# A graph layer: more columns copied by VectorE and ScalarE, and a wider repeated sum

## The chip, the core and the metric

The kernel runs on one core of one Trainium2 chip. The metric is the device time of one execution in microseconds. Five engines work beside each other and meet only through semaphores: PE (TensorE, matmuls; PEld is its weight load), DVE (VectorE), ACT (ScalarE), POOL (GpSimd), which here only issues gathers, and SP (SyncE), which only issues DMAs. A matmul writes PSUM, and only ACT and DVE read it out.

## What is computed

One layer of a graph network, a residual sum and a layer norm, for 12500 nodes of 64 numbers and 212500 edges, sorted by their destination, with 32 numbers each:

```
msg_in     = concat(nodes[src], nodes[dst], edge_features)      # 64 + 64 + 32
messages   = relu(msg_in @ mW1 + mb1) @ mW2 + mb2               # hidden width 128
aggregated = segment_sum(messages, dst)
u          = relu(concat(nodes, aggregated) @ uW1 + ub1) @ uW2 + ub2
out        = layernorm(nodes + u)
```

All of it is float32.

## The kernel before

The edges are cut into 554 groups of 384 (G), a group into three tiles of 128 (TG). Since the edges are sorted, the destinations of a group lie in a window of 32 nodes (W), whose start the kernel reads into a register.

Each group goes through three parts, and each part is matmuls on PE followed by reads of PSUM on ACT or DVE.

- **turn** (lines 354 to 379): the source rows of each tile, gathered by POOL into `own_s`, stand beside a one-hot of 32 columns for the place in the window, made by DVE (line 324). PE transposes both (line 360), and ACT copies the result into the block `own_st` (line 372), counting the edges of each place on the way.
- **hidden** (lines 381 to 409): PE multiplies the turned columns by `own_wm`, the first weights with the window's 32 rows in the middle (line 392), and ACT applies the relu into `own_h` (line 401).
- **sums** (lines 411 to 436): PE multiplies the hidden values of each tile by the one-hot (line 422), which adds them up by node: 128 hidden numbers by 32 nodes. The one-hot is broadcast four times (TIMES), so that PE makes the same 32 columns four times beside each other, 128 columns in all; only the first 32 are read. DVE adds them into `agg` (line 431) and the counts into a row of `xc` (line 432).

A float32 matmul is two instructions in the trace, each with a weight load.

The order is written out by hand. Iteration k (line 536) issues one step with turn(k), hidden(k-2) and sums(k-4), in this order on PE. Only the last matmul of a step raises PE's semaphore, and ACT and DVE wait for it. A step uses the PSUM buffer of k modulo 2, so step k+2 waits for what ACT and DVE read of step k. In each fourth step, those with k a multiple of 4, a further matmul (line 310) prepares the window rows of the next four groups and is then the last of its step; DVE copies the rows out (line 315, four copies). The last ten groups (SHORT) are issued part by part.

DVE's own order in an iteration is: the one-hot of group k+1, the adds of the step, and then column copies (below). So the one-hot that step k+2 needs is queued behind the column copies of iteration k.

**Gathers.** POOL gathers the rows of a tile with one indirect DMA (line 145). `own_s` is a ring of 20 groups; the gathers of a group wait for ACT's turn copy of the group 20 before. Iteration k issues those of group k+16.

**Column copies.** For some groups the third tile is not gathered. Instead its 128 source nodes are copied one column after the other out of `xc`, which holds all nodes transposed in SBUF, into a buffer `own_f`. `BY_DVE` lists the groups for which DVE does it (line 349), every 16th from 44: 31 groups. `BY_ACT` lists those of ACT (line 350), every 24th from 48: 21 groups. The 128 copies are spread over the 16 or 24 iterations that end 3 before the group is turned, 8 or 5.33 an iteration; the column numbers are read into eight registers at a time, one register load (line 343) for each eight copies. The hidden part of such a group has four matmul instructions in place of two for that tile: 64 rows from `own_f` padded with zeros, and the rest of the rows apart.

All 52 of these groups have numbers that are multiples of 4.

Updates of finished nodes (lines 438 to 485) are put between the steps, 512 nodes at a time.

Of the kernel before, what the change touches and what calls it, by code (L numbers as in the profile page):

```python
# [22 lines left out]
D = 64  # L23
# [5 lines left out]
W = 32  # L29
TG = 3  # L30
GE = TG * P
G = (E + GE - 1) // GE
# [11 lines left out]
NEAR_GROUPS = 24  # L44
SHORT = 10
ONE = TG - 1
BY_DVE = range(44, G - 16, 16)
BY_ACT = range(48, G - 16, 24)
COPIED = {**dict.fromkeys(BY_DVE, (ET.DVE, BY_DVE)), **dict.fromkeys(BY_ACT, (ET.Activation, BY_ACT))}
SLACK = 3  # L50
REGS = 8
TIMES = 4


def tiles_of(g):

    n = min(GE, E - g * GE)
    return [min(P, n - j * P) for j in range((n + P - 1) // P)]
# [23 lines left out]
class Own:  # L82
# [4 lines left out]
    def __init__(self, nc, ctx):  # L87
        def on(name, *shape, of=nc.sbuf_tensor):
            return ctx.enter_context(of(name, list(shape), F32)).ap()
# [6 lines left out]
        self.f = {way: [on(f"own_f{len(way)}_{i}", P, P) for i in range(2)]  # L96
                  for way in (BY_DVE, BY_ACT)}
        self.ident = on("own_ident", P, P)
# [6 lines left out]
def ordered(ctx: ExitStack, tc: tile.TileContext, a, own, ok):  # L105
# [25 lines left out]
    def after(first, *others):  # L131

        tc.declare_no_dep(first.ins, group="quiet", reason="waits for the last of a step")
        for i in others:
            tc.add_manual_dep(
                first.ins, i.ins.name,
                mybir.DependencyInfo(mybir.DependencyClass.Sync, mybir.DependencyReason.DATA),
                reason="the kernel's own rings",
            )
        return first  # L140
# [165 lines left out]
    def windows(b, wp, own_bank=True):  # L306


        xw, n = xws.pop(b)
        did = nc.tensor.matmul(wp[: n * W, :], xw[:, :n, :], w1b, start=True, stop=True)  # L310

        def copies():
            for i in range(n):
                g = b * SB + i
                c = nc.vector.tensor_copy(wm[g % NW][D : D + W, :], wp[i * W : (i + 1) * W, :])  # L315
                after(c, *([did] if own_bank else []), *([hidden_by[g - NW]] if g >= NW else []))
                wm_by[g] = c

        return did, copies
# [91 lines left out]
    def sums(g, ps):  # L411
        h, s = own.h[g % NH], own.s[g % RING]
        sizes = tiles_of(g)
        sg = ps[:, 2, : TIMES * W].rearrange("p (t w) -> p t w", w=W)


        lo = D if sizes[-1] == P else 0
        line = ps[0:1, 2, TIMES * W :][:, : D + W - lo]
        did = [nc.tensor.transpose(line, counts[lo:, g : g + 1], ident[lo : D + W, lo : D + W])]  # L419
        line = line[:, D - lo :]  # L420
        for j, p in enumerate(sizes):
            did.append(nc.tensor.matmul(  # L422
                sg, h[:p, j, :],
                s[:p, j, D:].unsqueeze(1).to_broadcast([p, TIMES, W]),
                start=j == 0, stop=j == len(sizes) - 1))

        def add(step):
            sums_by[g] = step
            at = bass.ds(starts.pop(g), W)
            return [  # L430
                after(nc.vector.tensor_tensor(agg[:, at], sg[:, 0, :], agg[:, at], ALU.add), step),  # L431
                after(nc.vector.tensor_tensor(xc[D : D + 1, at], line,  # L432
                                              xc[D : D + 1, at], ALU.add), step),
            ]

        return did, [*relu_by[g], copy_by[g]], add
# [53 lines left out]
    def step_update(g):  # L490
# [5 lines left out]
        elif now:  # L496
            got = now[1](now[0])
            now = [got, *now[2:]] if len(now) > 2 else []

    users = {part: [[], []] for part in (turn, hidden, sums)}  # L500

    def step(*work):
# [10 lines left out]
        for part, g, *_ in parts:  # L513
            if part is sums:
                for b in [b for b in xws if (b - 1) * SB <= g][:1]:
                    last, copies = windows(b, own.ps[g % 2][:, 2, (TIMES + 1) * W :][:, :H])
                    did.append(last)
# [18 lines left out]
    for k in range(G):  # L536
        if k < BITS:
            bit(k)
        if k % SB == 2:
            inputs(k // SB + 2)  # L540
        if k % SB == 1:
            places(k // SB + 1)
        onehot(k + 1)
        if k < G - SHORT:
            step((turn, k), *([(hidden, k - 2)] if k > 1 else []),
                 *([(sums, k - 4)] if k > 3 else []))
            made, summed = max(0, k - 1), max(0, k - 3)
        else:

            step((turn, k))  # L550
            for _ in range(2):
                if summed < made:
                    step((sums, summed))
                    summed += 1
            for _ in range(2):
                if made <= k:
                    step((hidden, made))
                    made += 1
        if k + AHEAD < G:
            gather(k + AHEAD)  # L560
        copies_of(k)
# [334 lines left out]
```

## Time and profile before

| | us |
|---|---|
| median of three runs | 2691.51 (2681.98 to 2695.5) |
| the profiled execution | 2690.72 |
| its span, first to last instruction | 2688.9 |
| mean granted clock of TensorE | 0.787 |

The span leaves 1.8 us of the profiled execution outside it. In that execution PE is busy 63% of the span, POOL 57%, DVE 39% and ACT 31%, so none is full. In the lines of the profile, L422 is line 422 of the kernel. A group line gives the line, the engine, the operation, output<-input, the count, the busy time and the mean of one in ns, and then the idle time of that engine just before such instructions and what ended it. A timeline line gives the start and the length in us; several equal instructions in a row are merged (x6), and the bracket names the idle time before the first. "issue" is idle time for which the profile shows no wait, and "remote" is a wait whose end the profile cannot name. The granted clock is 1.0 or 0.5 at each moment.

### The profile page before, as it was taken

The page shows a single profiled execution, that of the slowest core. Times are in us where ns is not written, and L with a number is a line of the kernel's source. Part 1 is how long each engine was busy: PE and PEld are TensorE (multiplying, and loading weights), DVE is VectorE, ACT ScalarE, POOL GpSimd, SP SyncE. Part 2 cuts the span into 40 slices and gives each one's busy share as a digit, 9 for nine tenths or more (in the row PEclk, how much of TensorE's full clock was granted, in tenths as well). Part 3 has the DMA queues.
Part 4 walks back from the last instruction along what each step waited for, and adds up shares of the span by engine and source line. Part 5 has one row for each costly group of instructions (what it writes and reads, how often), then busy time and mean ns, then how long its engine had stood idle before and what let it go on. Part 6 is the DMA issues. An engine that isn't in the chain of part 4 may idle for free.

```text
span 2688.9 us, 45023 instructions
## 1 busy us (share of the span) xinstructions
PE 1687.1 (63%) x9545; PEld 1457.1 (54%) x9545; DVE 1060.2 (39%) x7163; ACT 827.3 (31%) x4455; POOL 1519.4 (57%) x1616
## 2 busy tenths in 40 slices
PE   1356666666666675766666656666566666677667
PEld 0355555555555565655555555555555555565555
DVE  4124344344443444443434434434344343443423
ACT  0123333333333333333333333333333333333322
POOL 7565555555555555555555555555555555565550
PEclk9777787778777777777777878787777777787779
DMA  3211111111111111111111111111111111111110
GB/s 80 58 44 32 35 32 36 31 36 32 35 37 32 34 34 35 31 36 32 37 31 35 34 32 34 34 34 34 35 32 34 33 37 31 35 35 35 33 34 14
DMA packets 71878, 95.29 MB, mean 35 GB/s; under 512 B 32633, under 2 KB 40076, under 8 KB 71596
## 3 DMA queue, kind: packets, MB, share of 16 engines
q0 software_dynamic: 51488, 52.80, 10.3%
q1 hardware_dynamic: 19193, 39.06, 5.3%
q8 instruction: 81, 1.33, 0.2%
q14 instruction: 202, 1.65, 0.2%
q10 hardware_dynamic: 914, 0.46, 0.1%
HBM read 88.90 MB, written 3.20 MB: 34 GB/s over the span
## 4 chain that ended last, share of the span: by engine, by line
PE 50%; issue 18%; another core or an unknown queue 16%; ACT 10%; ACTq 3%; DVE 3%; DMA 0%; DVEq 0%; SPq 0%
PE own_ps L422 19%; PE own_ps L392 16%; PE own_ps L360 9%; ACT own_h L401 3%; ACT own_f L350 3%; ACT own_st L372 3%; ACTq L343 2%; PE own_ps L419 2%; PE u_ps L462 2%; PE u_ps L449 1%; PE own_ps L310 1%; ACTq L350 1%; PE u_ps L450 1%; DVE agg L431 1%
## 5 line engine op out<-in xcount | busy, mean ns | idle before, releaser
L145 POOL DMA_INDIRECT own_s<-in_x,src_sb x1609 | 1518.6, 944 | 1091.0 <-ACT own_st L372 677.1
L360 PE MATMUL own_ps<-own_ident,own_s 128*96 128x128 f32 x1661 | 364.2, 341 | 906.5 <-issue 677.0
L372 ACT ACTIVATE own_st<-own_ps 96x384 f32<-96x384 f32 (+2 forms) x606 | 286.1, 472 | 1697.7 <-PE own_ps L422 1006.0
L360 PEld LDWEIGHTS own_ps<-own_ident,own_s 128*96 128x96 f32 x1661 | 224.4, 159 | 983.9 <-issue 735.6
L422 PE MATMUL own_ps<-own_s,own_h 128*128 128x128 f32 x3322 | 647.5, 343 | 0.4 <-issue 0.3
L392 PE MATMUL own_ps<-own_wm,own_st 128*128 128x128 f32 (+1 forms) x3322 | 630.8, 338 | 1.4 <-DVE own_wm L315 1.4
L392 PEld LDWEIGHTS own_ps<-own_wm,own_st 128*128 128x128 f32 (+1 forms) x3322 | 571.9, 251 | 16.5 <-issue 11.7
L431 DVE TENSOR_TENSOR agg<-own_ps,agg 128x32 f32 x554 | 105.2, 190 | 1202.7 <-ACT own_h L401 1089.6
L422 PEld LDWEIGHTS own_ps<-own_s,own_h 128*128 128x128 f32 x3322 | 525.6, 236 | 27.3 <-issue 0.3
L349 DVE COPY own_f<-xc 64x1 f32 x3968 | 428.8, 143 | 217.7 <-issue 213.2
L350 ACT ACTIVATE own_f<-xc 64x1 f32 x2688 | 304.6, 193 | 9.1 <-issue 6.2
L401 ACT ACTIVATE own_h<-own_ps 128x384 f32<-128x384 f32 x553 | 263.3, 476 | 18.4 <-PE own_ps L392 13.1
L315 DVE COPY own_wm<-own_ps 32x128 f32<-32x128 f32 x550 | 156.9, 285 | 6.8 <-issue 1.3
L324 DVE TENSOR_TENSOR own_s<-iota,dlc 128x96 f32<-128x96 f32 x554 | 135.7, 245 | 21.6 <-issue 16.7
L432 DVE TENSOR_TENSOR xc<-own_ps,xc 1x32 f32 x554 | 101.2, 183 | 27.8 <-PE u_ps L450 7.4
L419 PE MATMUL own_ps<-own_ident,own_counts 32*1 32x32 f32 x554 | 107.1, 193 | 4.2 <-ACT own_st L372 1.9
L372 ACT ACTIVATION_READ_ACCUMULATOR own_st<-own_ps 96x1 f32 (+1 forms) x554 | 106.4, 192 | 0.6
L303 DVE COPY xw<-xc 66x32 f32 x554 | 78.6, 210 | 49.2 <-issue 48.3
L419 PEld LDWEIGHTS own_ps<-own_ident,own_counts 32*1 32x1 f32 x554 | 41.3, 74 | 93.8 <-issue 47.8
L310 PE MATMUL own_ps<-w1b,xw 66*128 66x128 f32 (+1 forms) x276 | 56.9, 290 | 0.0
L462 PE MATMUL u_ps<-u,u 128*128 128x64 f32 (+1 forms) x196 | 49.1, 398 | 10.0 <-ACT u L452 10.0
L462 PEld LDWEIGHTS u_ps<-u,u 128*128 128x128 f32 (+1 forms) x196 | 47.5, 326 | 11.5 <-ACT u L452 11.3
(63 smaller groups left out, 338.5 us busy)
## 6 DMA issues: line engine op xcount, KB each, us to landing
own_st<-in_efT SPq DMA_DIRECT2D x138, 192.0 KB
own_s<-in_x,src_sb POOLq DMA_INDIRECT x1609
xin<-in_x SPq DMA_DIRECT2D x24, 128.0 KB
out<-o SPq DMA_DIRECT2D x24, 128.0 KB
xc<-in_xT SPq DMA_DIRECT2D x12, 179.2 KB
dlc_i<-in_dst_cols SPq DMA_DIRECT2D x1, 831.0 KB
xc<-in_xT SPq DMA_DIRECT2D x4, 179.5 KB
src_sb<-in_src SPq DMA_DIRECT2D x13, 50.5 KB
```

The costliest lines, as they stand in the source:

```text
L145: nc.gpsimd.indirect_dma_start(out=s[:p, j, :D], out_offset=None, in_=x[:, :], in_offset=bass.IndirectOffsetOnAxis(ap=src_sb[:p, g * TG + ...
L315: c = nc.vector.tensor_copy(wm[g % NW][D : D + W, :], wp[i * W : (i + 1) * W, :])
L324: places_by[g] = nc.vector.tensor_tensor(own.s[g % RING][:, :, D:], iota.unsqueeze(1).to_broadcast([P, TG, W]), dlc[:, g * TG : (g + 1) * ...
L349: c = (nc.vector.tensor_copy(*column) if engine == ET.DVE else nc.scalar.activation(*column, AF.Copy))
L350: else nc.scalar.activation(*column, AF.Copy))
L360: nc.tensor.transpose(xt[:, j * P : j * P + p], s[:p, j, :], ident[:p, :p])
L372: nc.scalar.activation(t[to, c : c + m], xt[to, :m], AF.Copy, **({"accum_out": counts[to, g : g + 1]} if to.stop > D else {})), step)
L392: did.append(nc.tensor.matmul(pre[:p, j, :], edges, weights, start=i == 0, stop=i == len(parts) - 1))
L401: relu_by[g] = [nc.scalar.activation(h, pre, AF.Relu)]
L419: did = [nc.tensor.transpose(line, counts[lo:, g : g + 1], ident[lo : D + W, lo : D + W])]
L422: did.append(nc.tensor.matmul(sg, h[:p, j, :], s[:p, j, D:].unsqueeze(1).to_broadcast([p, TIMES, W]), start=j == 0, stop=j == len(sizes) - 1))
L462: nc.tensor.matmul(o_ps[:p, k], u[:, k:q:n], u2, start=True, stop=True)
```

## The change

```diff
-BY_DVE = range(44, G - 16, 16)
-BY_ACT = range(48, G - 16, 24)
+BY_DVE = range(44, G - 16, 12)
+BY_ACT = range(50, G - 16, 12)
 COPIED = {**dict.fromkeys(BY_DVE, (ET.DVE, BY_DVE)), **dict.fromkeys(BY_ACT, (ET.Activation, BY_ACT))}
 SLACK = 3
 REGS = 8
-TIMES = 4
+TIMES = 8
+FEW = 4
...
     def sums(g, ps):
         h, s = own.h[g % NH], own.s[g % RING]
         sizes = tiles_of(g)
-        sg = ps[:, 2, : TIMES * W].rearrange("p (t w) -> p t w", w=W)
+        times = TIMES if g < G - SHORT else FEW
+        sg = ps[:, 2, : times * W].rearrange("p (t w) -> p t w", w=W)
...
             did.append(nc.tensor.matmul(
                 sg, h[:p, j, :],
-                s[:p, j, D:].unsqueeze(1).to_broadcast([p, TIMES, W]),
+                s[:p, j, D:].unsqueeze(1).to_broadcast([p, times, W]),
                 start=j == 0, stop=j == len(sizes) - 1))
```

With G = 554 the new ranges hold 42 groups for DVE and 41 for ACT. DVE's are still multiples of 4; ACT's are 2 above a multiple of 4. Each engine's 128 copies are now spread over 12 iterations, 10.67 an iteration. The sums' matmuls have 256 columns in place of 128, but in the last ten groups, where they keep 128. The counts' row and the window rows move to later columns of the same PSUM bank.

## Prediction

> **What bounds it.** I first read the page's chain of the work that ended last and its costliest groups. Columns of a group line: line, engine, operation, output<-input, count | busy us, mean ns | idle before, releaser.
>
> ```profile
> PE 50%; issue 18%; another core or an unknown queue 16%; ACT 10%; ACTq 3%; DVE 3%; DMA 0%; DVEq 0%; SPq 0%
> L145 POOL DMA_INDIRECT own_s<-in_x,src_sb x1609 | 1518.6, 944 | 1091.0 <-ACT own_st L372 677.1
> L422 PE MATMUL own_ps<-own_s,own_h 128*128 128x128 f32 x3322 | 647.5, 343 | 0.4 <-issue 0.3
> L349 DVE COPY own_f<-xc 64x1 f32 x3968 | 428.8, 143 | 217.7 <-issue 213.2
> L350 ACT ACTIVATE own_f<-xc 64x1 f32 x2688 | 304.6, 193 | 9.1 <-issue 6.2
> ```
>
> The chain runs through PE for half the span, and for 16% through a wait that the profile can't name. Yet POOL's own row adds up to the span: 1518.6 busy and 1091.0 idle are 2609.6 us, and its last gather starts at 2610. Then the list of waits, for what POOL's idle time is:
>
> ```profile
> ACT own_st L372 <- PE own_ps L422: 1006.0, 245, 8.2
> POOL own_s L145 <- ACT own_st L372: 677.1, 274, 8.7
> ACT own_st L372 <- remote: 487.5, 78, 20.0
> ```
>
> POOL stops 274 times for ACT's turn copy, 2.47 us each, after 1609/274 = 5.9 gathers: two groups. So POOL does six gathers, stops with its ring full, and is freed by two turn copies. Third, the timeline of one such round of four groups:
>
> ```profile
> 1490.16 0.49 ACT L372 ACTIVATE own_st<-own_ps 96x384 f32<-96x384 f32 x1 [5.96 <-remote]
> 1491.01 0.94 POOL L145 DMA_INDIRECT own_s<-in_x,src_sb  x1 [2.40 <-ACT own_st L372]
> 1492.69 0.85 DVE L349 COPY own_f<-xc 64x1 f32 x8
> 1494.52 0.26 DVE L324 TENSOR_TENSOR own_s<-iota,dlc 128x96 f32<-128x96 f32 x1
> 1494.88 0.85 PE L360 MATMUL own_ps<-own_ident,own_s 128*96 128x128 f32 x3 [6.75 <-issue]
> ...
> 1496.00 0.94 POOL L145 DMA_INDIRECT own_s<-in_x,src_sb  x1 [0.30 <-issue]
> 1497.08 1.34 PE L422 MATMUL own_ps<-own_s,own_h 128*128 128x128 f32 x6
> 1498.45 0.49 ACT L372 ACTIVATE own_st<-own_ps 96x384 f32<-96x384 f32 x1 [5.48 <-PE own_ps L422]
> 1499.30 0.94 POOL L145 DMA_INDIRECT own_s<-in_x,src_sb  x1 [2.36 <-ACT own_st L372]
> 1503.63 0.39 PE L310 MATMUL own_ps<-w1b,xw 66*128 66x128 f32 x2
> 1505.54 0.94 POOL L145 DMA_INDIRECT own_s<-in_x,src_sb  x1 [0.30 <-issue]
> 1508.03 0.87 ACT L372 ACTIVATE own_st<-own_ps 64x256 f32<-64x256 f32 x2 [6.10 <-remote]
> ```
>
> The round has two halves. **Half A** (1490.16 to 1498.45): ACT frees PSUM, DVE works through adds, window rows and column copies up to the one-hot at 1494.52, PE begins at 1494.88 after 6.75 us of idleness, and ACT starts 0.03 us after PE's last sum. POOL had stopped by then, so this chain is on the path. **Half B** (1498.45 to 1508.03): PE's step ends with L310 at 1504.02, but ACT starts 4.0 us later. It starts 2.49 us after POOL's last gather began; of 205 such starts that came over 0.5 us after PE's end, the median is 2.42, half of them within 2.35 to 2.48. I can't say why ACT's release comes only with the end of POOL's burst; I take it as the trace shows it: half B lasts as long as POOL's six gathers and their landing, and PE has slack there.
>
> I counted this for groups 40 to 535. Steps k = 2 modulo 4 (half A): in 73 of 124 ACT starts within 0.1 us of PE's end (no slack), in the other 51 on average 1.26 us later. Steps k = 0 modulo 4 (half B): 3.43 us later on average, 2% without slack.
>
> **The change, part by part.** The sum is made against the profiled execution, 2690.72 us, which is 0.8 below the median of 2691.51, so no correction is due.
>
> *Fewer gathers.* 52 become 42 + 41 = 83 copied groups, so 31 gathers go (and 31 DMAs of POOL's queue). One costs 0.94 + 0.30 = 1.25 us of POOL's time (1491.01, 1492.26, 1493.50 in the timeline). What counts is in which half they go. A group's gathers wait for the turn copy 20 groups before, so groups 0 and 1 modulo 4 are gathered in half A, 2 and 3 in half B. All 52 were in A. Now DVE's 42 are in A and ACT's 41 in B. In B, where POOL is the limit: -41 x 1.25 = **-51 us**. In A 10 gathers more would cost 12 us if POOL limited it, but there the chain is late: 0.
>
> *DVE.* An iteration copies 10.67 columns in place of 8. Eight take 0.96 us, 0.145 the last, so one each 0.116: +0.31 us. Register loads rise from 1 to 1.33 an iteration; one takes 0.608 us (L343 on DVE's queue) and nothing runs on DVE meanwhile, with about 0.65 between copies: +0.21. Together 0.52 us ahead of the one-hot. In A it is on the path, in B below the slack.
>
> *ACT.* 5.33 become 10.67 copies of 0.097 (x6 take 0.66), loads of 0.55 rise from 0.67 to 1.33: +0.9 us an iteration. They stand behind the relu, so PE's next step does not wait; the second turn copy of a pair does, which POOL needs 3.75 us after the first and has now after some 1.4. Hidden; without that cover 0.9 us a half. No wait is added: the copies of a group begin 15 iterations before it, into a buffer whose last reader, the hidden part of the group 24 before, was issued seven iterations earlier.
>
> *Sums.* The trace has no 256-column matmul. Six of 128 columns begin 0.213 us apart at half clock and 0.112 at full clock (L392 x6 takes 1.49 and 0.83). The nearest row that is wider is the update's, with 512 columns, at half clock:
>
> ```profile
> 1414.06 1.91 PE L449 MATMUL u_ps<-agg,wc 128*128 128x512 f32 x2
> ```
>
> Two start 0.85 apart, four times 0.213, so the time goes with the columns. Six matmuls gain 128 columns each: +1.28 us at half and +0.67 at full clock. Were the weight load the limit (236 ns mean in L422's PEld row) it could be nothing; and it could be below nothing, if denser work brought the full clock earlier: a step takes 3.84 us in A (median) and 2.15 where the clock is full. Bounds for A: -1.0 (all of A's step at full clock: -1.69 + 0.67) and +1.28. I take +1.03, since A's step starts cold after 5.6 us of idleness (median) and two thirds of these steps run at half clock to their end; with a longer step some of the rest falls after the turn to full.
>
> *Together in A*: 0.52 + 1.03 = 1.55 us. 73 of 124 pay it whole, 51 have 1.26 of slack and pay 0.3: 0.59 x 1.55 + 0.41 x 0.3 = 1.04 us, in about 130 rounds: **+135 us**. Ten fewer groups in A have the two extra hidden matmuls, 4.57 against 3.84 us a step: **-7**. *In B* the second step of the pair ends about 0.6 to 1.3 us later, and POOL needs its turn copy 3.75 us after the first one; by its spread (median 2.9, upper tenth 3.75 us) only the late ones overrun, some 0.15 us a round: **+20**. The last ten groups are unchanged.
>
> Sum: 2690.7 - 51 - 7 + 135 + 20 = **2788 us**, 3.6% slower.
>
> [...] Gathers that ran beside at least 0.4 us of DVE's column copies took 944 ns (478 of them), those beside none 944 ns too (933), so the sum has nothing for it. [...] The clock in the table by stages is 0.61 in 1490 to 1495 and 0.50 in 1510 to 1515, where PE idles, and 1.00 in 1500 to 1505. [...]
>
> **Rivals.** (1) *POOL alone decides, faster.* If A's step reaches full clock early or PE's wider sums hide behind the burst, all that is left is the gathers: 31 x 1.25 = 39 us, 51 at most: **2640 to 2652**, taken as 2647. It holds if A's chain grows by under about 0.3 us on the whole. For it: none of DVE, ACT and PE is above 63%, and a denser PE could raise the clock. Against: 73 steps without slack. (2) *PE becomes the bound, much slower.* If no step profits from the full clock and B's slack is used up too, A costs 1.28 + 0.52 = 1.8 in all 130 rounds (+234) and B 0.3 (+40), less 51: **2914**. (3) *The parts cancel*: A pays only DVE's 0.52 with 0.59 of the rounds (+40) against -51: **2680**, no difference. That the change does not do what it says is excluded by the ranges: 83 groups are copied.
>
> **How the numbers follow.** Forecast 2788 (own range 2725 to 2860): 0.50. Rival 1: 0.28. Rival 2: 0.12. Rival 3: 0.10. The range from 2638 to 2880 reaches to rival 1 and to most of rival 2. One measurement can tell about 0.5% (13 us) from no change. Faster by more: 0.29; within: 0.10; slower: 0.61.
>
> **What would show it.** Right: gathers 1578; L422 with 128x256 in two pitches near 0.22 and 0.43; ACT's start in half A directly after L422, POOL's stops there longer by over 1 us and as many as before; in B the unnamed wait smaller. Wrong: a mean clock well above 0.787 with A's step at full clock; POOL's stops unchanged at 2.4 us; or stops after three gathers in place of six.

## The result, and the profile after

The changed kernel takes 2841.12 us (median of 4 runs, 2836.41 to 2850.73), the kernel before on the same chip 2690.07: a ratio of 1.0569, 95% interval 1.053 to 1.0608. So it is slower by 151 us, where 97 were forecast. All lines of the profile after stand one or two lines lower than in the kernel before (L145 is now L146, L372 is L373, L422 is L424).

The chain of the work that ended last, and the groups of gathers, sums and column copies, in the page after:

```profile
PE 46%; issue 20%; ACT 11%; another core or an unknown queue 11%; ACTq 4%; DVE 2%; DVEq 0%
L146 POOL DMA_INDIRECT own_s<-in_x,src_sb x1578 | 1493.8, 947 | 1258.1 <-ACT own_st L373 837.0
L424 PE MATMUL own_ps<-own_s,own_h 128*128 128x256 f32 (+1 forms) x3322 | 1046.6, 460 | 0.0
L350 DVE COPY own_f<-xc 64x1 f32 x5376 | 587.4, 144 | 541.2 <-issue 527.7
```

POOL's row adds up to the span again, and this is the quickest way to read the loss: 31 gathers fewer make it busy for 24.8 us less, its idle time grows by 167.1 (1091.0 to 1258.1), and the difference, 142.3, is nearly all of the 145.8 us by which the span grew. The unnamed wait fell from 16% to 11% of the chain, and time in which an engine waits for nothing that the profile shows rose from 18% to 20%. The list of waits after (engine, what it waited for: us in all, times, longest):

```profile
POOL own_s L146 <- ACT own_st L373: 837.0, 304, 8.9
ACT own_st L373 <- PE own_ps L424: 729.4, 199, 7.5
ACT own_st L373 <- remote: 422.5, 93, 20.8
```

POOL stops 304 times for 2.75 us each, where it was 274 times for 2.47. One half A of the changed kernel, from the timeline (start, length, and in brackets the idle time before):

```profile
1489.91 1.18 DVE L316 COPY own_wm<-own_ps 32x128 f32<-32x128 f32 x4
...
1491.13 0.57 DVE L350 COPY own_f<-xc 64x1 f32 x8
...
1492.30 0.26 DVE L350 COPY own_f<-xc 64x1 f32 x2 [0.60 <-issue]
1492.95 0.52 DVE L304 COPY xw<-xc 66x32 f32 x4 [0.39 <-issue]
...
1493.50 0.26 DVE L325 TENSOR_TENSOR own_s<-iota,dlc 128x96 f32<-128x96 f32 x1
...
1493.86 0.85 PE L361 MATMUL own_ps<-own_ident,own_s 128*96 128x128 f32 x3 [4.47 <-issue]
...
1496.78 2.93 PE L424 MATMUL own_ps<-own_s,own_h 128*128 128x256 f32 x6
...
1499.74 0.49 ACT L373 ACTIVATE own_st<-own_ps 96x384 f32<-96x384 f32 x1 [6.97 <-PE own_ps L424]
...
1500.59 0.95 POOL L146 DMA_INDIRECT own_s<-in_x,src_sb  x1 [4.09 <-ACT own_st L373]
```

A register load now falls between DVE's column copies (the 0.60 us before the last two), and the sums take 2.93 us in place of 1.34. ACT starts directly after PE's last sum, and POOL has stood still for 4.09 us.

The whole kernel by halves, means in us over the groups 40 to 535 of each trace. A half runs from ACT's turn copy of one step to that of the step two later; where a group has copied columns, ACT makes two turn copies, and the half counts from the end of both. A half is cut into the time until PE starts that later step, PE's step, and what ACT still waits after PE's end.

| | half A: to PE, PE, wait | sum | half B: to PE, PE, wait | sum |
|---|---|---|---|---|
| before | 4.80 + 3.92 + 0.54 | 9.25 | 3.62 + 2.62 + 3.46 | 9.70 |
| after | 5.52 + 4.74 + 0.45 | 10.70 | 4.16 + 3.40 + 1.83 | 9.39 |

Half A is longer by 1.45 us, half B shorter by 0.31; 1.14 times some 137 rounds of four groups is 156 us, a little more than the 146 by which the span grew. Of the 1.45 us, 0.16 is the first of two turn copies, which 41 groups now have at the end of half A (with two, ACT reads the counts 0.88 us after it starts, with one 0.39). In half B the longer chain only used up ACT's wait.

### The profile page after: what moved, and what is told of

It is laid out like the page before. It is cut to its first block, busy times and chain, and to the rows that moved or that the text cites. A ratio compares the mean times of both kernels' runs of the same rounds, so it can differ in the third digit from the quotient of the medians.

```text
span 2834.7 us, 53542 instructions
## 1 busy us (share of the span) xinstructions
PE 2007.9 (71%) x9607; PEld 1594.9 (56%) x9607; DVE 1216.0 (43%) x8571; ACT 1116.5 (39%) x7046; POOL 1494.5 (53%) x1585
## 3 DMA queue, kind: packets, MB, share of 16 engines
q8 instruction: 81, 1.33, 0.2%
## 4 chain that ended last, share of the span: by engine, by line
PE 46%; issue 20%; ACT 11%; another core or an unknown queue 11%; ACTq 4%; DVE 2%; DVEq 0%
PE own_ps L424 23%; PE own_ps L393 12%; PE own_ps L361 7%; ACT own_f L351 6%; ACT own_st L373 3%; ACTq L344 3%; ACT own_h L402 2%; PE own_ps L421 1%; PE own_ps L311 1%; PE u_ps L464 1%; ACTq L351 1%; PE u_ps L451 1%; PE u_ps L452 1%; DVE stats L470 1%
## 5 line engine op out<-in xcount | busy, mean ns | idle before, releaser
L146 POOL DMA_INDIRECT own_s<-in_x,src_sb x1578 | 1493.8, 947 | 1258.1 <-ACT own_st L373 837.0
L424 PE MATMUL own_ps<-own_s,own_h 128*128 128x256 f32 (+1 forms) x3322 | 1046.6, 460 | 0.0
L373 ACT ACTIVATE own_st<-own_ps 96x384 f32<-96x384 f32 (+2 forms) x637 | 298.6, 469 | 1484.8 <-PE own_ps L424 729.4
L361 PE MATMUL own_ps<-own_ident,own_s 128*96 128x128 f32 x1661 | 338.0, 321 | 756.7 <-issue 601.9
L350 DVE COPY own_f<-xc 64x1 f32 x5376 | 587.4, 144 | 541.2 <-issue 527.7
L424 PEld LDWEIGHTS own_ps<-own_s,own_h 128*128 128x128 f32 x3322 | 695.0, 225 | 118.8
L351 ACT ACTIVATE own_f<-xc 64x1 f32 x5248 | 567.3, 193 | 74.6 <-issue 67.4
L393 PE MATMUL own_ps<-own_wm,own_st 128*128 128x128 f32 (+1 forms) x3322 | 580.4, 316 | 0.7 <-DVE own_wm L316 0.7
L393 PEld LDWEIGHTS own_ps<-own_wm,own_st 128*128 128x128 f32 (+1 forms) x3322 | 517.2, 229 | 17.1 <-issue 7.6
L373 ACT ACTIVATION_READ_ACCUMULATOR own_st<-own_ps 96x1 f32 x554 | 106.5, 192 | 1.0
L311 PEld LDWEIGHTS own_ps<-w1b,xw 66*128 66x128 f32 (+1 forms) x276 | 57.3, 208 | 9.3
```

Of the source, the lines that this page charges most:

```text
L146: nc.gpsimd.indirect_dma_start(out=s[:p, j, :D], out_offset=None, in_=x[:, :], in_offset=bass.IndirectOffsetOnAxis(ap=src_sb[:p, g * TG + ...
L350: c = (nc.vector.tensor_copy(*column) if engine == ET.DVE else nc.scalar.activation(*column, AF.Copy))
L351: else nc.scalar.activation(*column, AF.Copy))
L361: nc.tensor.transpose(xt[:, j * P : j * P + p], s[:p, j, :], ident[:p, :p])
L373: nc.scalar.activation(t[to, c : c + m], xt[to, :m], AF.Copy, **({"accum_out": counts[to, g : g + 1]} if to.stop > D else {})), step)
L393: did.append(nc.tensor.matmul(pre[:p, j, :], edges, weights, start=i == 0, stop=i == len(parts) - 1))
```

## The experiments

The theory after the result: the chain of half A (DVE's copies, then PE's step) pays everything that the change adds to it, and half B, held by POOL's burst, pays nothing and gains a little from fewer gathers. The rivals are in the expectations. The first four runs each do one part of the change, on one chip, where the kernel before took 2680.64 us (13 runs).

**Only the sums eight times.**

```diff
-TIMES = 4
+TIMES = 8
+FEW = 4
...
```

The lines of `sums` are as in the change.

> The kernel before with the eightfold sums alone (fourfold in the last ten groups), copies as before. Theory 1, chain in half A with no slack to absorb it: PE's step in half A grows by 0.82 to 1.03 us in each of some 137 rounds of four groups, and all of it shows: 112 to 140 us more, 2800 to 2830. Theory 2, chain in half A with the slack counted in the prediction (51 of 124 steps absorb 1.26 us): 0.6 of that, 67 to 85 us more, 2757 to 2775. Theory 3, PE as the bound everywhere: the sums' own busy time, 1046.6 less 647.5, 399 us more, 3090. Theory 4, POOL alone decides: no difference, 2690.

Measured: 2762.66 us, ratio 1.0316 (1.0272 to 1.0359), so +82; granted clock 0.848, as in the whole change. By halves: A 4.74 + 4.84 + 0.28, B 3.56 + 3.06 + 3.02. PE's step in A is 0.92 longer, of which ACT's wait there takes up 0.26. Theory 2, with the slack, holds to its number.

```profile
L424 PE MATMUL own_ps<-own_s,own_h 128*128 128x256 f32 (+1 forms) x3322 | 1022.0, 451 | 1.8 <-issue 1.8
```

The mean clock rises from 0.787 to 0.848 and the kernel still gets slower: the sums' busy time alone grows from 647.5 to 1022.0 us.

**Only the new groups to copy.**

```diff
-BY_DVE = range(44, G - 16, 16)
-BY_ACT = range(48, G - 16, 24)
+BY_DVE = range(44, G - 16, 12)
+BY_ACT = range(50, G - 16, 12)
```

> The kernel before with the new copy ranges alone (42 groups by DVE, 41 by ACT), sums four times. Theory 1 (half A's chain, nothing absorbed): DVE's part ahead of the one-hot grows by 0.52 to 0.72 us in each of 137 rounds, 71 to 99 us more, less 51 us for 41 gathers in half B: 20 to 48 us more, 2710 to 2738. Theory 2 (slack absorbs two fifths): 42 to 59 more less 51: 2681 to 2699, no difference. Theory 4 (POOL alone): 31 gathers of 1.25 us less, 2651.

Measured: 2753.55 us, ratio 1.0254 (1.0219 to 1.0289), +73, more than any of the theories said. With the sums' +82 that makes 155, against 151 for the change: the two parts add, and the copies were the part that I had wrong.

**Only DVE's groups.**

```diff
-BY_DVE = range(44, G - 16, 16)
+BY_DVE = range(44, G - 16, 12)
```

> The kernel before with DVE's copies alone raised to 42 groups; ACT's stay 21 groups at multiples of 4, sums four times. All 63 groups lie in half A, so half B gains nothing. Theory 1: 0.52 to 0.72 us of DVE in each round, 71 to 99 us more: 2761 to 2789. Theory 2 (two fifths absorbed, and some of the 11 gathers felt): 35 to 55 us more, 2725 to 2745. Theory 4 (POOL alone): 11 gathers fewer, 14 us less, 2676.

Measured: 2762.68 us, ratio 1.031 (1.0273 to 1.0348), +82, though 11 gathers are gone; theory 1's range holds. By halves: A 5.64 + 4.10 + 0.17, B 4.08 + 2.63 + 2.94. The time to PE's start in half A grows by 0.84 us, where 0.52 were forecast. Following DVE through half A shows why. Before, eight copies take 0.60 us from the first start to the last end (mean; the 0.85 in the prediction's round is one of the longest), because the register load (0.608 us) and most register operations run ahead while the four window rows are copied (1.18 us). With 10.67 columns an iteration the loads of eight no longer fall on the start of an iteration, and the columns take 1.40 us, 0.40 of it gaps where a load stands between two copies. These gaps are half of the 0.80 us by which the stretch grew. The columns themselves are the other half: in the 42 of 124 rounds in which no load stands between them, they still take 1.17 us. The eight of the kernel before start 0.060 us apart; the last ones of ten or eleven, and those behind a load, 0.115.

**Only ACT's groups.**

```diff
-BY_ACT = range(48, G - 16, 24)
+BY_ACT = range(50, G - 16, 12)
```

> The kernel before with ACT's copies alone raised to 41 groups and moved to 2 above a multiple of 4; DVE's stay 31 groups, sums four times. Theory 1: ACT's copies stand behind the relu and off the path, half B loses 41 gathers (51 us less), half A has 21 groups fewer with the two extra hidden matmuls (15 us less) and its bursts 21 gathers more where POOL limits (0 to 26 us more): 2625 to 2655, faster. Rival: ACT's copies delay the second turn copy of a pair, so POOL stops after three gathers and the gain is used up: 2690 or more, with many more bursts of three gathers than the 38 of before.

Measured: 2668.59 us, ratio 0.9952 (0.9934 to 0.997), -12. By halves: A 5.14 + 3.82 + 0.88 (9.84), B 3.56 + 2.88 + 2.55 (8.99). Half B gains more than the 41 gathers that left it (0.71 us, some -97 in all), and half A loses most of it (0.59, +81). The time lies between theory 1 and the rival. With the +82 of DVE's groups it makes 70, near the 73 of both.

```profile
L145 POOL DMA_INDIRECT own_s<-in_x,src_sb x1589 | 1499.9, 944 | 1095.1 <-ACT own_st L372 666.5
```

POOL's row says it in short: 18.7 us less busy, 4.1 us more idle. I sorted POOL's stops by the turn copy that ended them. The table has what they last beyond the usual pitch of 1.25 us between gathers, for the groups 40 to 535:

| us (stops) | after the first turn copy of a pair, B and A | after the second |
|---|---|---|
| before | 239 (108) and 225 (109) | 90 (53) |
| only the sums | 242 (112) and 308 (116) | 67 (49) |
| only DVE's groups | 247 (110) and 309 (123) | 80 (48) |
| only ACT's groups | 194 (92) and 212 (112) | 159 (89) |
| the change | 226 (114) and 381 (122) | 123 (86) |

With ACT's groups the stops for the second turn copy of a pair grow by 69 us, and those for the first shrink by 58. The rival says that ACT's own column copies, which stand ahead of the second turn copy, take the gain back. The trace does not show that. Of 248 pairs, 79 have the second turn copy over 3.75 us after the first (45 before), but in only 13 of them was ACT at work until then. In 55 it had stood idle, PE's step had ended over 0.5 us before, and it started 2.44 us (median) after POOL's last gather had begun: the late release that the prediction found in half B.

The same release holds up DVE in half A. In 33 of 124 rounds DVE stands idle for 2.2 us directly before the one-hot, with no wait that the profile shows (16 rounds and 1.0 us before), and 29 of these one-hots start 2.1 to 2.45 us after POOL's last gather began. That is 0.46 us a round more than before; the first of two turn copies in the 41 groups adds 0.16. One such round, in which the one-hot starts 2.41 us after the last gather:

```profile
741.09 0.94 POOL L145 DMA_INDIRECT own_s<-in_x,src_sb  x1 [0.30 <-issue]
743.50 0.26 DVE L324 TENSOR_TENSOR own_s<-iota,dlc 128x96 f32<-128x96 f32 x1 [2.12 <-issue]
...
743.75 0.49 ACT L372 ACTIVATE own_st<-own_ps 96x384 f32<-96x384 f32 x1 [4.38 <-DVE own_s L324]
```

I read it so: when half B gets shorter, POOL's burst ends in half A and holds that up instead. No run on such a chip parts it further. Bursts of three gathers in place of six rise from 38 to 61 (to 109 in the whole change).

**ACT's copies without their gathers, and the reverse.** To part the two, POOL's list of left-out gathers was cut loose from ACT's list of copies.

```diff
+LEFT = {*BY_DVE, *range(48, G - 16, 24)}
...
-            for j, p in enumerate(tiles_of(g)) if not copied(g, j)
+            for j, p in enumerate(tiles_of(g)) if not (g in LEFT and j == ONE)
```

This stands beside ACT's new range; in the second kernel `BY_ACT` is as before, and `LEFT` holds `range(50, G - 16, 12)` beside DVE's groups.

> ScalarE copies the 41 new groups' columns (50, 62, ...) as in e4_act, but POOL gathers exactly what it gathered before: the last tiles of groups 48, 72, ... are left out of the gathers (so those 21 groups are computed with stale sources), and those of 50, 62, ... are gathered although nothing reads them. So ScalarE's work of e4_act stands alone. e4_act measured -12 us where the prediction had -51 -7. Theory S (the gathers are worth what was predicted, and the added instructions of ScalarE take it back by making VectorE's one-hot late in half A, 4.82 against 4.43 us after ScalarE's turn copy in e4_act): +30 to +45 us. Theory G (ScalarE's copies are hidden as predicted, and a gather left out in half B is worth far less than 1.25 us): 0 to +10 us, one-hot at 4.4 to 4.5 us.

> The other half: ScalarE copies what it copied before (groups 48, 72, ...), and POOL leaves out the gathers that e4_act left out (last tiles of 50, 62, ..., whose 41 groups are then computed with stale sources; the last tiles of 48, 72, ... are gathered and not read). 1588 gathers or one more, as in e4_act. Theory S: -40 to -60 us, one-hot in half A at 4.4 to 4.5 us. Theory G: -8 to -20 us.

These two, and the next two, came to a chip on which the kernel before takes 2039.7 us (13 runs, 2038.64 to 2042.42), so they answer another question than the one put. ACT's copies alone: 2040.13 us, ratio 1.0002 (0.9993 to 1.0012). Fewer gathers alone: 2015.6, ratio 0.9883 (0.9867 to 0.99), -24, which is 20 gathers at 1.2 us. The gathers' group on the page of ACT's copies alone:

```profile
L146 POOL DMA_INDIRECT own_s<-in_x,src_sb x1609 | 1520.4, 945 | 491.4 <-issue 369.1
```

The same kernel's list of waits, for POOL:

```profile
POOL own_s L146 <- issue: 369.1, 1211, 0.3
POOL own_s L146 <- ACT own_st L373: 10.1, 33, 0.3
```

The gathers are the same 1609 and take the same 945 ns as on the first chip, but POOL never stops: no wait for ACT is longer than 0.3 us, and 1520.4 + 491.4 = 2011.8 of a span of 2035.1 us. ACT starts 0.22 us after PE's end in half B (mean), not 3.46, and no wait is left unnamed. On this chip POOL sets the time of the kernel before (20 gathers fewer bring 24 us); a stop that isn't there can't grow, so what ACT's copies cost on the first chip is not tested by this.

**Sixteen columns to a register load.**

```diff
-REGS = 8
+REGS = 16
```

with DVE's new range as in the third run.

> e3_dve (VectorE's copies in every 12th group, +82 us) with 16 columns to a register load in place of 8, on both engines: 0.67 loads an iteration of VectorE in place of 1.33. Theory L (a load, during which VectorE runs nothing, is most of VectorE's term: in e3_dve the one-hot came at 4.45 us before the change, 5.00 with one load and 5.67 with two): +10 to +40 us against before, one-hot in half A at 4.5 to 4.9 us on average. Theory C (the columns themselves and the instructions that must be fetched for them): +65 to +85 us, one-hot above 5.1 us.

Measured, on the other chip: 2260.79 us, ratio 1.1085 (1.106 to 1.111), +221. The one-hot of half A comes 5.48 us after ACT's turn copy. Theory L is not confirmed: the one-hot is later than with DVE's groups and loads of eight on the first chip (5.27), since a load of sixteen is also longer; neither theory gave the time (columns: fastest, median and slowest in ns):

```profile
L343 DVEq TENSOR_LOAD <-cols_sb x336: 1095/1120/1379, 120.8 to 2169.4; - x168
```

In the kernel before it is 593/608/802. What the longer load alone costs isn't settled, as DVE's range alone did not run on this chip.

**No gathers from group 40 on.**

```diff
-            for j, p in enumerate(tiles_of(g)) if not copied(g, j)
+            for j, p in enumerate(tiles_of(g)) if not copied(g, j) and g < 2 * RING
```

> The kernel before with all gathers from group 40 on left out (the sources are then stale, all other work is the same). Theory B (half B lasts as long as POOL's burst and its landing): ScalarE's wait after PE's end in half B falls from 3.46 us to below 0.5, the unnamed waits nearly vanish, half B shrinks from 9.70 to 6.3 to 7.0 us, half A stays between 8.5 and 9.3, and the time is 2230 to 2330 us. Rival (the late release is PE's or ScalarE's own, whatever POOL does): the wait stays above 2 us in half B and the time stays above 2560 us.

Measured on the other chip, one run: 1989.6 us. ACT waits 0.27 us in half B. The drop is only 50 us, as no late release is there to go away, so the expectation was put to a chip that can't answer it. What it gives is the length of PE's, DVE's and ACT's chain with no POOL at all: 7.79 + 6.39 us a round, 1990 us.

**The changed kernel on the other chip, and without gathers.** The first is the changed kernel as it is, the second has the edit just shown.

> The changed kernel once more, because the last four runs showed that the kernel before takes 2039.7 us on one chip (POOL never stops, ScalarE starts within 0.3 us of PE's end in both halves) and 2680.6 us on another. If this chip is like the one of the prediction (before near 2690): 2825 to 2860 us, as measured. If it is like the other (before near 2040): Theory C (there PE's and VectorE's chain of 14.2 us a round is the limit, just above POOL's 1609 x 1.25 us, so all that the change adds to the chain in both halves is paid, and the 31 gathers fewer give nothing): 2300 to 2430 us, ratio 1.13 to 1.19. Rival P (there POOL is the limit, the chain has room): 2000 to 2100 us.

> The changed kernel with all gathers from group 40 on left out (stale sources, all other work the same); beside e8_nogather it gives the change to PE's, VectorE's and ScalarE's chain alone. Theory C: within 40 us of e9_after_again if that runs near 2300 to 2430; and 2280 to 2420 us too, over 400 us below e9_after_again, if this chip is like the one of the prediction (there half B ends only when POOL's burst has landed, and without gathers that wait goes: the unnamed waits vanish). Rival (the late release of ScalarE in half B has nothing to do with the gathers): on such a chip above 2700 us, with the unnamed waits still there. Rival P: below 2100 us.

Both came to the other chip. With gathers 2393.98 us, ratio 1.1745 (1.1724 to 1.1766), without them 2392.43 (one run). Theory C holds to both its numbers, and Rival P falls: here the chain is everything, and leaving out all gathers changes the time by under 2 us. Without gathers half A grows from 7.79 to 9.48 us and half B from 6.39 to 7.86. So both halves pay, where on the first chip only A did; that is why the same change costs 17% here and 6% there. With gathers, the chain of the work that ended last:

```profile
PE 68%; issue 14%; ACT 11%; ACTq 4%; DVE 3%; DMA 0%; DVEq 0%
```

And the waits of ACT's turn copy and of POOL:

```profile
ACT own_st L373 <- PE own_ps L424: 739.3, 317, 7.5
POOL own_s L146 <- ACT own_st L373: 413.6, 270, 5.3
```

There is no unnamed wait, and PE's share of the chain is 68%.

**All registers of an iteration in one load**, in the changed kernel, ahead of its first copy.

```diff
-            for r in range(at * P // way.step, (at + 1) * P // way.step):
-                if r % REGS == 0:
-                    _, ahead[:] = nc.values_load_multi_w_load_instructions(
-                        cols_sb[n : n + 1, r : r + REGS], engines=[engine], min_val=0,
...
+            turns = range(at * P // way.step, (at + 1) * P // way.step)
+            _, ahead[:] = nc.values_load_multi_w_load_instructions(
+                cols_sb[n : n + 1, turns.start : turns.stop], engines=[engine], min_val=0,
...
+            for r in turns:
-                column = f[:D, r : r + 1], xc[:D, bass.ds(ahead[r % REGS], 1)]
+                column = f[:D, r : r + 1], xc[:D, bass.ds(ahead[r - turns.start], 1)]
```

> The changed kernel, but each iteration loads the registers of all its 10 or 11 columns at once, ahead of the first copy, on both engines; all else as in the change. In the kernel before the eight columns of half A take 0.60 us from the first start to the last end (the load and the register operations run ahead while the four window rows are copied); in the changed kernel 10.67 columns take 1.40 us, 0.40 of it where a load falls between two of them. Theory L (VectorE's term is a load in the middle): 0.75 to 0.95 us, one-hot in half A at 4.5 to 4.7 us after ScalarE's turn copy in place of 5.1 to 5.2; the time falls by 60 to 140 us against the changed kernel: 2255 to 2335 where that takes 2394 (before 2036), 2730 to 2790 where it takes 2841 (before 2690). Theory C (the columns themselves cost it): still 1.25 us or more, time within 25 us of the changed kernel's.

Measured on a chip like the first (before 2685.79 us): 3021.09 us, ratio 1.1256 (1.1233 to 1.128), worse than the change itself. Neither theory gave that. The register loads of DVE's and ACT's queues, columns as above:

```profile
L343 DVEq TENSOR_LOAD <-cols_sb x504: 5/2517/2856, 220.0 to 2924.0; - x168
L343 ACTq TENSOR_LOAD <-cols_sb x492: 987/2413/2541, 247.5 to 2892.5; - x164
```

One iteration of DVE in half A, from the timeline of this kernel:

```profile
1503.22 1.18 DVE L316 COPY own_wm<-own_ps 32x128 f32<-32x128 f32 x4
...
1505.96 1.30 DVE L350 COPY own_f<-xc 64x1 f32 x11 [1.55 <-issue]
```

A load of eleven registers takes 2.57 us (median of 336), one of ten 1.08 (of 168); the copies of window rows no longer cover it, and DVE stands 1.55 us before its first column. The one-hot comes at 6.08 us, where it was 5.16. So a load that nothing covered cost time here, 1.55 us of its 2.57, and this price was unknown to me; theory L's remedy is refuted. That the load is all of DVE's term is refuted too: with it ahead of the first copy, the columns still take 1.33 us.

**ACT's groups alone, with such loads on ACT:** the same edit, with DVE's range and the sums as before.

> The attempt at a kernel better than both: only ScalarE's new range (e4_act, 72 copied groups, sums of four), with whole loads on ScalarE (VectorE's are whole already). On the chip where before takes 2036 POOL's 1609 gathers set the time there, and 20 gathers left out alone gave -24 us (e6_gathers), ScalarE's copies alone 0 (e5_actwork): 2005 to 2025 us if both add, 2030 to 2050 if ScalarE's copies and the fewer gathers meet in PE's chain (1990 us without any gathers). Where before takes 2690: 2640 to 2672 us (e4_act -12).

Measured on that chip: 2674.73 us, ratio 0.9961 (0.9946 to 0.9976), -11, as with ACT's groups alone, and just above the range expected. ACT's loads of 2.4 us move POOL's stops from the first turn copies (266 us) to the second (293) and leave the sum. ACT's groups alone, 0.5% below the kernel before, is the best version that I have; it beats both kernels on the first kind of chip and did not run on the other.

## Why the prediction was right in sign and short by 54 us

- **The chain of half A.** Predicted 0.52 + 1.03 = 1.55 us; in the change its two parts grew by 0.72 and 0.82, in all 1.54. That the sum agrees is luck: DVE's part is larger than forecast, the sums' smaller. The sums' term holds roughly (0.92 alone, and +82 us, where 0.59 of 1.03 us in 137 rounds is 83). DVE's does not (0.84 alone).
- **DVE's term** went wrong at "eight take 0.96 us". That row is from half B. In half A the same eight end 0.60 us after the first starts, because their load is hidden under the copies of window rows (it begins with them and takes 0.608 of their 1.18 us), so "nothing runs on DVE meanwhile" does not hold there. Of the 0.80 us by which the stretch grew, 0.40 are gaps at a load, where the sum has 0.21, and 0.40 are the columns, where it has 0.31. The load that was hidden came out, and so did register operations that had run ahead.
- **The step that failed** is "51 have 1.26 of slack and pay 0.3". With DVE's groups alone or the sums alone, ACT's wait in half A does shrink, by 0.37 and 0.26 us, together 0.63, which is 0.41 of 1.55. With ACT's groups alone it grows by 0.34, and in the whole change it falls only from 0.54 to 0.45. So half A paid 1.45 us of 1.54, +199 us where I had +128 (135 less 7). 0.16 us of the wait is no waiting but the first of two turn copies, a cost on the path for which the sum has nothing; without it the whole change absorbs 0.25 us, half of the 0.51 that I took. For the other half the traces show only this: the slack was no reserve of the chain but the late release. In 41 of the 51 rounds ACT started over 0.5 us after PE's end, and 2.39 us (median) after POOL's last gather had begun, as in half B. With ACT's groups alone there are 52 such rounds, and 14 in the change. So this slack depends on where POOL's bursts end.
- **ACT's term**, "Hidden", is not shown to be wrong. I had named the price of a late second turn copy and put it at 20 us for PE alone, without ACT's own copies; its stops rose from 53 to 86 and by 33 us. But of the 59 pairs in which the second copy came over 3.75 us after the first, ACT had been at work until then in 9.
- **Fewer gathers and half B.** Predicted -51 + 20 = -31 us, measured -0.31 us in 137 rounds, -42. Near in sum; the two terms were not measured apart. Alone, ACT's groups were expected to bring at least 35 us (2655 against 2690) and brought 12: the gain of half B is given back in half A, most of it before the one-hot, which comes 0.37 us later (4.77 against 4.40) though DVE's work is unchanged, and in the second turn copy of 41 groups.
- **The rivals.** POOL alone (2647) fails: its stops grew. POOL sets the time only on the other chip, and there only of the kernel before. The parts do not cancel (2680). The result lies between the forecast and rival 2 (2914), which was nearer in half A (nearly every round pays, 199 us against its 234) and wrong in half B.
- **The signs.** As predicted: 1578 gathers; sums 0.216 and 0.427 us apart; ACT directly after L424; POOL's stops of half A longer by over 1 us (2.06 to 3.12) and about as many (109 and 122); ACT's wait in half B smaller. Of the marks against, the clock rose to 0.849, but half A's step did not come to full clock (its mean clock is 0.61, and 0.56 before); and more bursts did end after three gathers.
- **Gathers and the clock.** Gathers took 944 ns before and 947 after, beside 1408 more column copies, so it was right that the sum has nothing for gathers beside copies. The mean clock rose with wider sums, from 0.787 to 0.848 for the sums alone, but it was no guide to the time, which rose by 82 us.

## What to carry to other kernels

A small instruction that is free because another covers it (here a register load of 0.608 us behind copies of 1.18 us) can stop being free when its place in the order shifts (here 0.40 us of gaps a round): before changing how often something is done, see whether the new count still divides evenly into the buffers and loads that now hide it. Slack that is counted in the kernel before belongs to the wait that makes it; if the change touches what makes that wait (here the place where POOL's bursts end), the slack can't be counted on: of the 0.51 us a round that I took, 0.25 was there. And where a wait has no name in the profile, a gain that rests on it may hold on one chip only: run both kernels on another before trusting the size (the change here cost 5.7% on one chip and 17.5% on another).

## What the chips showed that I had not expected

The same kernel took 2680.6, 2685.8 and 2690.1 us on some chips and 2039.7 and 2036.4 us on another, with gathers of 944 and 945 ns. Before against ACT's copies alone on the other chip, which has the same 1609 gathers, half B takes 9.70 against 6.52 us, all of it ACT's wait (3.46 against 0.22), and half A 9.25 against 7.95, most of it PE's step (3.92 against 3.03; the mean clock is 0.787 against 0.888). On the first kind DVE also shows register operations of over 0.3 us, most of about 0.7 (40 of them before, 298 in the changed kernel); on the other there is none. The traces of the first kind also hold far fewer semaphore events (13002 before, against 35468 for ACT's copies alone on the other), so that a wait has no name there says less than its length. The cause of the difference stays open. That the late release is tied to the landing of POOL's burst is argued from the times (before: 2.42 us after the last gather began, whose last packet ends 2.12 us after that in the median); the run without gathers that would show it did not meet such a chip.

Register loads did not take time in proportion to their length: on DVE 0.35 us for four (line 296) and 0.61 for eight in the kernel before, 1.08 for ten and 2.57 for eleven with all registers in one load, and 1.12 for sixteen on the other chip.
